# A graph layer on one core: transform the second half of the batches to frequencies on two row groups of TensorE

## The chip, the cores and the metric

The kernel runs on one core of a Trainium2 chip. The metric is the device time of one execution in microseconds; the kernel before takes 1838.17 us (median of four runs, 1836.39 to 1841.95). A core has TensorE (matmuls, in the profile PE, and its weight loads, PEld), VectorE (DVE), ScalarE (ACT), GpSimd (POOL) and SyncE (SP, which here only issues DMAs). ScalarE and POOL issue DMAs too. All data are 32-bit floats.

## The reference

For 32 batches of 512 tokens and 256 features the layer normalises the rows, `h = max(layernorm(x), 0)`, and computes from `h`, cut to what matters here:

```python
g = relu(bn1(conv1(h)))              # 1x1 convolution over the channels
g = bn2(conv2(g))                    # 17 taps along the tokens, 256 -> 256 channels
x_conv = relu(g + h)
s = h @ w_se.T + b_se                # 3 features
A = exp(-dist(s, s)) * adj           # 512 x 512 per batch
x_nmp = A @ relu(h @ w_msg.T + b_msg)
r, z, n = gru_gates([x_conv, x_nmp], h)
out = x + (1 - z) * n + z * h
```

The convolution with 17 taps is done in frequencies: the tokens are cut into windows of 64, each is transformed to 80 real numbers, multiplied by the transformed taps and transformed back.

## The kernel before

The batches form two groups of 16. `V = 64` is the window, `L = 80` the numbers per transformed window, `W = 8` the windows of a batch, so one group fills 128 columns (`W * GB`) of a tile `xf` of 128 channels x 2 channel halves x 80 frequencies x 128 windows.

The work runs in five stages: the first part for group 0 (0 to about 160 us), the node stage of group 0 (messages, distances, aggregation, with the products of the frequencies between), the first part for group 1 (about 456 to 576 us), the node stage of group 1, and the gates for all pairs of batches (from about 870 us).

`first_part(g, ...)` (from L806) is a loop over the batches of a group, written by hand inside `manual_schedule`, so the order of the calls is the order on each engine's queue. Per batch b it runs, in a skewed pipeline: `statistics(b + 2)` and `normalise(b + 2)` on VectorE with a power on POOL, `transpose_h(b + 1)` (8 transposes on TensorE, L311, two evictions on VectorE, L315, a DMA to HBM), `conv1(b)` (8 matmuls of 256 columns, each two passes in the trace, L327; VectorE adds the shift, L330; ScalarE does the relu, L331) and `windows_to_freq(b - 1)`.

`windows_to_freq` (L335 to L346) takes, for each half of the channels, four blocks of 128 tokens as weights, `H1[b][:, c, ...]` (128 tokens x 128 channels), and multiplies them by the constant `fwd`, 128 x 160. `fwd` is block diagonal: rows 0 to 63 with columns 0 to 79 transform the even window, rows 64 to 127 with columns 80 to 159 the odd window. Two blocks share a PSUM bank, and ScalarE copies it, four windows of 80, into `xf` (L345).

In group 0 the loop also transforms the taps. `weights_to_freq` (L245 to L269) is one of 32 steps: four matmuls of 17 rows, 80 weight columns and 512 columns, one on each row group of 32 rows (L255), each into a bank of its own; the banks are copied to SBUF, two or three of the four by ScalarE (L265), the others by VectorE (L263), and every second step four DMAs on SP's queue store them to HBM (L269). Which engine copies which bank depends on the place of the step in its group of four input channels: in a step that begins such a group VectorE takes banks 1 and 3, in the other it takes bank 3 alone. `load_taps` loads the inputs of four steps, on POOL's queue.

`between(b)` gives the steps of a batch and `slot()` places them: for most batches one step after the transposes and one after `conv1`, with a third after `windows_to_freq` in two batches; batch 1 has none of its own and does what batch 0 left. Every PSUM tile is one of 8 banks, given out in turn, so a matmul waits until the copies of the bank's last user are done. Group 1 has no taps; there `between` gives sums of the gates' weights on POOL and ScalarE.

The gates end with `last_z` for the last pair of batches, whose output is stored by four DMAs of 128 KB for the first batch and two times four of 64 KB for the second, by turns on SP's and ScalarE's queues (`store`, L808).

Of the kernel before, what the change touches and what calls it, by code (L numbers as in the profile page):

```python
# [15 lines left out]
P = 128  # L16
# [8 lines left out]
V = 64  # L25
# [40 lines left out]
def gnn_layer(  # L66
# [268 lines left out]
    def windows_to_freq(b, xf):  # L335
        w0 = (b % GB) * W
        per = 2
        for ic in range(DC):
            for c0 in range(0, NC, per):
                p = bank(f"px_{b}_{ic}_{c0}")  # L340
                for j in range(per):
                    nc.tensor.matmul(p[:, j * 2 * L : (j + 1) * 2 * L], H1[b][:, c0 + j, ic * P : (ic + 1) * P],  # L342
                                     fwd, start=True, stop=True)
                w = w0 + 2 * c0
                nc.scalar.copy(xf[:, ic, :, w : w + 2 * per],  # L345
                               p[:, : per * 2 * L].rearrange("p (w f) -> p f w", f=L))  # L346
        del H1[b]
# [62 lines left out]
    def load_h(b):  # L410
        HT[b] = work.tile([P, DC, N], FP, tag="hT", name=f"hT2_{b}")
        nc.sync.dma_start(HT[b], HD[b])
# [240 lines left out]
    def last_z(p, terms):  # L653

        d, o, ks = RZ[p], 1, range(K3)

        def gated(src, other, i, j, t=slice(0, N)):
            z, g = d[:, DC + i, j, t], DC + i
            if other is not None:
                nc.vector.tensor_add(z, other[:, t], src[:, t])  # L660
                src = z
            nc.scalar.activation(z, src, AF.Sigmoid, bias=brz[:, g : g + 1], scale=1.0)

        def places(i, t):
            return slice(t.start // 32, t.stop // 32), slice(32 * i, 32 * (i + 1))

        def turned(i, j, t=slice(0, N)):
            dst, (js, half) = d[:, i, j, t], places(i, t)
            nc.vector.tensor_mul(dst, dst, d[:, DC + i, j, t])
            if (p, j) not in OUT:  # L670
                OUT[p, j] = pools["late"].tile([P, N // 32, D // 4], FP, tag="o", name=f"o_{p}_{j}", bufs=2)
            nc.vector.transpose(OUT[p, j][:, js, half], dst.rearrange("p (j k) -> p j k", k=32))

        def added(i, j, t=slice(0, N)):
            js, half = places(i, t)
            x = XP[p][j][:, js, half]
            nc.vector.tensor_add(x, x, OUT[p, j][:, js, half])


        ts = [slice(h * N // 2, (h + 1) * N // 2) for h in range(2)]  # L680
        b1, b2, b4, *b3 = (bank(f"pz{k}_{p}") for k in range(1, 6))
        into(b1, Q1, o, ks, terms, True)
        p1 = temp("p1", f"z{p}")
        nc.scalar.copy(p1, b1)
        into(b2, Q6, o, ks, terms, True)
        u2 = temp("u2", f"z{p}")
        nc.vector.tensor_add(u2, p1, b2)
        into(b1, Q2, o, ks, terms, False)
        gated(b1, None, 0, 0)
        early_out(p, 1, 1)  # L690
        turned(0, 0)
        into(b2, Q7, o, ks, terms, False)
        u3 = temp("u3", f"z{p}")
        nc.vector.tensor_add(u3, p1, b2)
        early_out(p, 0, 1)
        added(0, 0)
        for bk, t in zip(b3, ts):
            into(bk, Q5, o, ks, terms, True, t)
            gated(bk, u3, 1, 1, t)
        into(b4, Q4, o, ks, terms, True)  # L700
        turned(1, 1)
        added(1, 1)
        gated(b4, u3, 1, 0)
        for bk, t in zip(b3, ts):
            into(bk, Q3, o, ks, terms, False, t)
            gated(bk, u2, 0, 1, t)
            if t is ts[0]:
                turned(1, 0)
        added(1, 0)
        store(p, 0, [nc.sync, nc.scalar])  # L710
        for t in ts:
            turned(0, 1, t)
            added(0, 1, t)
            store(p, 1, [nc.sync, nc.scalar], t)
# [100 lines left out]
    def first_part(g, freq, between, left=()):  # L815


        b0, b1 = g * GB, (g + 1) * GB
        for b in range(b0, b0 + 3):
            if b not in X and (g == 0 or b == b0):  # L820
                load_x(b)
        if g == 0:
            t = XN[b0] = pools["first"].tile([P, NC, D], FP, tag="xn", name="rows", bufs=2)
            ones, diags = t[:, 0, :P], t[:, 1:3, :].rearrange("p i (c m) -> p i c m", m=P)
            nc.vector.memset(ones, 1.0)

            for _ in range(5):
                nc.tensor.matmul(row1[1][:, : 2 * P], ident, fr.rearrange("p c g k -> p (c g k)")[:, : 2 * P], start=True, stop=True)
            batch_norm("bn1", scale1, shift1, nc.gpsimd)
            bn1_row(0, scale1, ones, diags)  # L830
            bn1_row(1, shift1, ones, diags)
        if b0 not in STATS:
            statistics(b0)
        normalise(b0)
        if g == 0:
            scale_w1()
            shift_w1()
        left = list(left)

        def fill():  # L840
            for step in left.pop(0) if left else ():
                step()

        if g > 0:
            load_x(b0 + 1)
            fill()
            load_x(b0 + 2)
        transpose_h(b0)
        fill()
        statistics(b0 + 1)  # L850
        if g > 0:
            statistics(b0 + 2)
        normalise(b0 + 1, g > 0)
        fill()
        for b in range(b0, b1):
            if b + 3 < b1:
                load_x(b + 3, nc.gpsimd)
            if b == b0:
                conv1(b)
                one, two = between(0) if g == 0 else ([], [])  # L860
                for step in one:
                    step()
                fill()
                if g == 0:
                    transpose_h(b + 1)
                    statistics(b + 2)
                    normalise(b + 2)
                else:
                    normalise(b + 2)
                    transpose_h(b + 1)  # L870
                fill()
                xf, last_two = freq(g), two
                continue
            if g == 0:

                slots = last_two if b == b0 + 1 else between(b - b0)

                def slot():
                    for step in slots.pop(0) if slots else ():
                        step()  # L880

                if b == b0 + 1:
                    between(b - b0)
                    conv1(b)
                    slot()
                if b == b0 + 2:
                    slot()
                if b == b1 - 1:
                    load_h(b0)
                if b + 2 < b1:  # L890
                    statistics(b + 2)
                if b + 1 < b1:
                    transpose_h(b + 1)
                if b > b0 + 2:
                    slot()
                if b + 2 < b1:
                    normalise(b + 2)
                if b > b0 + 1:
                    conv1(b)
                    slot()  # L900
                if b == b1 - 1:
                    by_chunks(b)
                    load_h(b0 + 1)
                windows_to_freq(b - 1, xf)
                slot()
                continue
            if b + 2 < b1:
                statistics(b + 2)
            if b + 1 < b1:
                transpose_h(b + 1)  # L910
            if b + 2 < b1:
                normalise(b + 2)
            one, two = between(b - b0)
            conv1(b)
            if b == b1 - 1:
                load_h(b0)
            for step in one:
                step()
            windows_to_freq(b - 1, xf)
            for step in two:  # L920
                step()
        if g > 0:
            by_chunks(b1 - 1)
            load_h(b0 + 1)
        windows_to_freq(b1 - 1, xf)
        by_chunks(b0)
        return xf
# [8 lines left out]
    with tc.tile_pool(name="freq", bufs=1) as fpool:  # L936
# [3 lines left out]
        with phase("first", "gen"):  # L940
# [10 lines left out]
            nc.scalar.dma_start(fwd, nc.inline_tensor(fwd_np, name="dft_fwd").ap())  # L951

            def between(b):
                if 1 <= b <= len(load_weights):
                    load_weights[b - 1]()

                n = (2, 0, *(3 if b in (6, 11) else 2 for b in range(2, GB)))[b]
                mine = [[steps.pop(0)] for _ in range(n)]
                if b % 2 == 0 and b // 2 + 1 < QI // PI:
                    mine[b > 0].insert(0, partial(load_taps, gen, b // 2 + 1))  # L960
                return (mine[0], mine[1:]) if b == 0 else mine

            with tc.manual_schedule():
                xf = first_part(0, freq_tile, between)
# [159 lines left out]
```

## Time and profile before

| what | value |
|---|---|
| four runs | median 1838.17 us, 1836.39 to 1841.95 |
| the profiled execution | 1841.95 us, span 1840.2 us |
| granted TensorE clock | 0.995 of full speed |
| first part, group 0 (0 to 160 us) | TensorE busy 153.67 us, VectorE 119.65, ScalarE 85.52, DMA 0.90 |
| node stage, group 0 (160 to 456 us) | TensorE busy 292.79 us of 296, DMA 0.79 |
| first part, group 1 (456 to 576 us) | TensorE busy 120.00 us of 120, VectorE 97.64, ScalarE 50.50, DMA 0.69 |
| node stage, group 1 (576 to 870 us) | TensorE busy 293.28 us of 294, DMA 0.83 |
| gates (870 to 1840 us) | TensorE busy 958.60 us of 970, DMA 0.35 |

The profiled execution is one of the four runs, and the slowest of them. In the lines that follow, a timeline line gives the start in us, the length in us from the first start to the last end of a run of equal instructions, engine, line, operation and tiles, how many, and in brackets the idle time before it with what ended it. A busy TensorE is no proof of full use, since matmuls are pipelined and overlap in the records: the distance from one start to the next is the better measure. A line of instructions by tile gives how many and the shortest, median and longest duration in ns.

### The profile page before, as it was taken

The page shows a single profiled execution, that of the slowest core. Times are in us where ns is not written, and L with a number is a line of the kernel's source. Part 1 is how long each engine was busy: PE and PEld are TensorE (multiplying, and loading weights), DVE is VectorE, ACT ScalarE, POOL GpSimd, SP SyncE. Part 2 cuts the span into 40 slices and gives each one's busy share as a digit, 9 for nine tenths or more (in the row PEclk, how much of TensorE's full clock was granted, in tenths as well). Part 3 has the DMA queues.
Part 4 walks back from the last instruction along what each step waited for, and adds up shares of the span by engine and source line. Part 5 has one row for each costly group of instructions (what it writes and reads, how often), then busy time and mean ns, then how long its engine had stood idle before and what let it go on. Part 6 is the DMA issues. An engine that isn't in the chain of part 4 may idle for free.

```text
span 1840.2 us, 20110 instructions
## 1 busy us (share of the span) xinstructions
PE 1818.3 (99%) x6614; PEld 1083.9 (59%) x6614; DVE 1107.5 (60%) x2220; ACT 583.5 (32%) x1084; POOL 590.5 (32%) x572
## 2 busy tenths in 40 slices
PE   8999999999999999999999999999999999999997
PEld 6776666666897766675545554555445554555443
DVE  7884556554896555454266456654666456655666
ACT  4555343432345333333212221222122221222121
POOL 3431233334432444444331332123221323133221
PEclk9999999999999999999999999999999999999999
DMA  9998789775678987877432344224422443234412
GB/s 238 312 294 225 224 239 240 201 205 182 202 250 202 261 254 217 231 209 235 113 100 50 90 120 120 71 50 120 120 86 36 119 120 103 56 82 120 120 26 44
DMA packets 307500, 289.26 MB, mean 157 GB/s; under 512 B 148076, under 2 KB 237196, under 8 KB 307012
## 3 DMA queue, kind: packets, MB, share of 16 engines
q1 hardware_dynamic: 281380, 224.22, 45.8%
q10 hardware_dynamic: 18992, 38.68, 5.9%
q0 software_dynamic: 7024, 25.07, 4.5%
q8 instruction: 53, 0.87, 0.2%
q14 instruction: 51, 0.42, 0.1%
HBM read 191.50 MB, written 96.40 MB: 156 GB/s over the span
## 4 chain that ended last, share of the span: by engine, by line
PE 91%; DMA 3%; DVE 2%; issue 1%; ACT 1%; POOL 1%; SPq 0%; ACTq 0%; DVEq 0%; POOLq 0%
PE pg L601 30%; PE pn L601 15%; PE pn L491 12%; PE py L392 11%; PE pc L327 5%; PE pm L439 5%; PE pc L589 5%; PE px L342 3%; PE pd L476 2%; PE pw L255 1%; PE phT L311 1%; DMA adj<-in_adj_dram 1%; PE pz L601 1%; DMA x<-in_x_dram 1%; PE psr L465 1%
## 5 line engine op out<-in xcount | busy, mean ns | idle before, releaser
L491 PE MATMUL pn<-A,msg 128*128 128x512 f32 x512 | 227.4, 597 | 2.5 <-ACT e L479 2.1
L601 PE MATMUL pg<-hp,sw 128*128 128x512 f32 x434 | 221.8, 593 | 0.7 <-DVE rz L620 0.5
L601 PE MATMUL pg<-cp,sw 128*128 128x512 f32 x434 | 221.6, 592 | 0.0
L601 PE MATMUL pg<-np,sw 128*128 128x512 f32 x434 | 221.6, 592 | 0.0
L579 POOL TENSOR_TENSOR hp<-hp 128x512 f32<-128x512 f32 x64 | 81.3, 1281 | 414.4 <-DMA hp<-hd 295.3
L491 PEld LDWEIGHTS pn<-A,msg 128*128 128x128 f32 x512 | 97.4, 191 | 114.0 <-issue 106.8
L371 POOL TENSOR_TENSOR both<-xf 128x256 f32<-128x256 f32 x78 | 60.0, 769 | 324.9 <-PE py L392 290.4
L579 POOL TENSOR_TENSOR cp<-cp 128x512 f32<-128x512 f32 x64 | 80.5, 1268 | 228.0 <-ACT cp L595 226.8
L392 PE MATMUL py<-wt,both 128*128 128x256 f32 x624 | 152.4, 387 | 0.3 <-ACT e L479 0.3
L616 ACT ACTIVATE rz<-rz,brz 128x512 f32<-128x512 f32 x93 | 67.0, 721 | 260.2 <-DVE rz L620 260.2
L399 DVE TENSOR_TENSOR y<-y,py 128x256 f32<-128x256 f32 x78 | 31.8, 408 | 186.3 <-ACT y L398 186.3
L601 PEld LDWEIGHTS pg<-hp,sw 128*128 128x128 f32 x434 | 82.2, 190 | 104.8 <-issue 98.3
L601 PEld LDWEIGHTS pg<-np,sw 128*128 128x128 f32 x434 | 82.5, 190 | 103.8 <-issue 103.8
L601 PEld LDWEIGHTS pg<-cp,sw 128*128 128x128 f32 x434 | 82.5, 190 | 103.8 <-issue 103.8
L392 PEld LDWEIGHTS py<-wt,both 128*128 128x128 f32 x624 | 115.1, 192 | 43.4 <-issue 27.6
L482 DVE TENSOR_TENSOR A<-e,at 128x512 f32<-128x512 f32 x128 | 115.4, 940 | 34.7 <-ACT e L479 34.5
L358 POOL TENSOR_TENSOR wsum<-wt 128x512 f32<-128x512 f32 x78 | 108.7, 1395 | 54.7 <-DMA wt<-wd 42.8
L327 PE MATMUL pc<-w,hT 128*128 128x256 f32 x512 | 119.5, 387 | 1.5 <-DVE hT L315 1.5
L739 ACT ACTIVATE nt<-nt,vech 128x512 f32<-128x512 f32 x64 | 46.2, 722 | 235.8 <-DVE nt L738 235.8
L439 PE MATMUL pm<-wmsg,hq 128*128 128x259 f32 x512 | 117.5, 381 | 0.0
L601 PE MATMUL pn<-np,sw 128*128 128x512 f32 x224 | 114.4, 592 | 0.0
L601 PE MATMUL pn<-hp,sw 128*128 128x512 f32 x224 | 114.4, 592 | 0.0
(145 smaller groups left out, 2945.6 us busy)
## 6 DMA issues: line engine op xcount, KB each, us to landing
wt<-wd SPq DMA_DIRECT2D x160, 256.0 KB, 4.5
adj<-in_adj_dram SPq DMA_DIRECT2D x128, 256.0 KB, 5.6
wd<-wst SPq DMA_DIRECT2D x64, 320.0 KB, 6.0
yd<-y ACTq DMA_DIRECT2D x80, 256.0 KB, 4.2
yt<-yd SPq DMA_DIRECT2D x30, 640.0 KB, 7.4
hd<-hT SPq DMA_DIRECT2D x32, 512.0 KB, 4.4
nd<-nmp ACTq DMA_DIRECT2D x32, 512.0 KB, 4.4
xb<-in_x_dram SPq DMA_DIRECT2D x128, 128.0 KB, 3.8
```

The lines of the kernel that those rows point to most:

```text
L327: nc.tensor.matmul(p[:, j, :], HT[b][:, ic, c * P : (c + 1) * P], w1[:, ic, :], start=(ic == 0), stop=(ic == DC - 1))
L342: nc.tensor.matmul(p[:, j * 2 * L : (j + 1) * 2 * L], H1[b][:, c0 + j, ic * P : (ic + 1) * P], fwd, start=True, stop=True)
L358: nc.gpsimd.tensor_tensor(t, WT[g, u][:, 0], WT[g, u][:, 1], op=ALU.add)
L371: nc.gpsimd.tensor_tensor(both[:, 0], re, im, op=ALU.add)
L392: nc.tensor.matmul(dst, v[:, ic, :], w[:, ic, :], start=(ic == 0), stop=(ic == DC - 1))
L439: nc.tensor.matmul(p[:, : D + NS], hq[:, ic, c * P : (c + 1) * P], wmsg[:, ic, :], start=(ic == 0), stop=(ic == DC - 1))
L482: nc.vector.tensor_mul(A[b][:, mc, :], e, at)
L491: nc.tensor.matmul(p, MSG[b][:, mc, dc * P : (dc + 1) * P], A[b][:, mc, :], start=(mc == 0), stop=(mc == NC - 1))
L579: nc.gpsimd.tensor_tensor(t[:, dst, :], t[:, a, :], t[:, b, :], op=sub)
L589: nc.tensor.matmul(bk[:, t0:t1], YT[p][j][:, c, oc * P : (oc + 1) * P], back[:, n : n + t1 - t0], start=(c == 0), stop=(c == len(spans) - ...
L601: nc.tensor.matmul(bk[:, t], sw[:, k, q, o, :], terms[k][q][:, t], start=(first and i == 0), stop=(i == len(ks) - 1), skip_group_check=True)
L616: nc.scalar.activation(rz[:, g, j, :], src, AF.Sigmoid, bias=brz[:, g : g + 1], scale=1.0)
```

## The change

Three things change.

In group 1 (b of 16 or more) `windows_to_freq` takes each half of a token block by itself: 64 rows of `H1` as weights, 80 columns of `fwd`, rows 0 to 63 into one bank for the even windows and rows 64 to 127 into another for the odd ones. Per half of the channels there are eight matmuls of 64 rows and 80 columns by turns on the two row groups in place of four of 128 rows and 160 columns. ScalarE copies each bank once, into every second window of `xf`. Group 0 keeps the old matmuls.

In group 0 the slots are gone. Both groups run one loop body: statistics, transposes, normalise, `conv1`, the first step of the batch, `windows_to_freq`, the other steps. The 32 steps are spread over 15 batches (two each, three in batches 7 and 14, none in batch 15), the last `by_chunks` and `load_h` come after the loop in both groups, and `load_taps` is called before the steps of every even batch.

In `last_z` the four stores of the last pair's first batch all go to SP's queue.

```diff
     def windows_to_freq(b, xf):
         w0 = (b % GB) * W
         per = 2
-        for ic in range(DC):
+        for ic in range(DC) if b >= GB else ():
+
+            ps = [bank(f"px_{b}_{ic}_{k}") for k in range(2)]
+            for c in range(NC):
+                for k, p in enumerate(ps):
+                    rows = slice(V * k, V * (k + 1))
+                    nc.tensor.matmul(p[:, c * L : (c + 1) * L], H1[b][rows, c, ic * P : (ic + 1) * P],
+                                     fwd[rows, k * L : (k + 1) * L], start=True, stop=True)
+            for k, p in enumerate(ps):
+                nc.scalar.copy(xf[:, ic, :, w0 + k : w0 + W : 2],
+                               p[:, : NC * L].rearrange("p (w f) -> p f w", f=L))
+        for ic in range(DC) if b < GB else ():
             for c0 in range(0, NC, per):
...
-        store(p, 0, [nc.sync, nc.scalar])
+        store(p, 0, [nc.sync])
...
-            if g == 0:
-
-                slots = last_two if b == b0 + 1 else between(b - b0)
...
-                windows_to_freq(b - 1, xf)
-                slot()
-                continue
+            if g == 0 and b == b0 + 1:
+                conv1(b)
+                for step in last_two:
+                    step()
             if b + 2 < b1:
                 statistics(b + 2)
             if b + 1 < b1:
                 transpose_h(b + 1)
             if b + 2 < b1:
                 normalise(b + 2)
             one, two = between(b - b0)
-            conv1(b)
+            if b > b0 + (g == 0):
+                conv1(b)
             if b == b1 - 1:
                 load_h(b0)
             for step in one:
                 step()
             windows_to_freq(b - 1, xf)
             for step in two:
                 step()
-        if g > 0:
-            by_chunks(b1 - 1)
-            load_h(b0 + 1)
+        by_chunks(b1 - 1)
+        load_h(b0 + 1)
         windows_to_freq(b1 - 1, xf)
...
             def between(b):
+                if b % 2 == 0 and b // 2 + 1 < QI // PI:
+                    load_taps(gen, b // 2 + 1)
                 if 1 <= b <= len(load_weights):
                     load_weights[b - 1]()
-
-                n = (2, 0, *(3 if b in (6, 11) else 2 for b in range(2, GB)))[b]
-                mine = [[steps.pop(0)] for _ in range(n)]
-                if b % 2 == 0 and b // 2 + 1 < QI // PI:
-                    mine[b > 0].insert(0, partial(load_taps, gen, b // 2 + 1))
-                return (mine[0], mine[1:]) if b == 0 else mine
+                mine = spread(steps, b, GB - 1) if b < GB - 1 else []
+                return mine[:1], mine[1:]
```

More of the change, by code (lines that the diff above doesn't have):

```diff
@@ L873, in first_part @@
                 continue
-            if g == 0:
-                slots = last_two if b == b0 + 1 else between(b - b0)
[L878 to L883, printed above, removed]
-                    conv1(b)
-                    slot()
[L886 to L902, printed above, removed]
-                    load_h(b0 + 1)
-                windows_to_freq(b - 1, xf)
-                slot()
-                continue
+            if g == 0 and b == b0 + 1:
+                conv1(b)
+                for step in last_two:
+                    step()
             if b + 2 < b1:
@@ L913, in first_part @@
             one, two = between(b - b0)
-            conv1(b)
+            if b > b0 + (g == 0):
+                conv1(b)
             if b == b1 - 1:
@@ L921, in first_part @@
                 step()
-        if g > 0:
-            by_chunks(b1 - 1)
-            load_h(b0 + 1)
+        by_chunks(b1 - 1)
+        load_h(b0 + 1)
         windows_to_freq(b1 - 1, xf)
```

## The prediction

> **What bounds the kernel now.** I read the page first: engine totals and the chain of work that ended last.
>
> ```profile
> span 1840.2 us, 20110 instructions
> PE 1818.3 (99%) x6614; PEld 1083.9 (59%) x6614; DVE 1107.5 (60%) x2220; ACT 583.5 (32%) x1084; POOL 590.5 (32%) x572
> PE 91%; DMA 3%; DVE 2%; issue 1%; ACT 1%; POOL 1%; SPq 0%; ACTq 0%; DVEq 0%; POOLq 0%
> ```
>
> TensorE is the bound, so a microsecond counts where the TensorE stream gets shorter or gets a new hole. Second, the frequency matmuls by tile (px), the edited step:
>
> ```profile
> L342 PE MATMUL px<-fwd,h x512: 299/299/403, 26.4 to 572.5; 128*128 128x160 f32 x171
> L345 ACT COPY xf<-px x128: 406/438/485, 27.9 to 573.0; 128x320 f32<-128x320 f32 x128
> ```
>
> The file has 256 such matmuls and the trace 512: each runs as two passes. The longest record is 403 ns, 104 more than the median: a first pass that had to wait for its weights. So a load of 128 columns costs about 0.104 us when nothing hides it. Third, the timeline of the second group (482 to 490 us):
>
> ```profile
> 483.08 2.34 PE L342 MATMUL px<-fwd,h 128*128 128x160 f32 x16
> 485.26 1.04 PE L311 MATMUL phT<-ident,xn 128*128 128x128 f32 x8
> 489.59 2.34 PE L342 MATMUL px<-fwd,h 128*128 128x160 f32 x16
> ```
>
> Read start to start: px to phT is 2.18 us for 16 passes, 0.136 each, and a batch is 6.51 us without a hole. Fourth, matmuls that already use row groups, the distances (pd, 9 rows by 128 columns of weights) and the taps (pw, 17 rows, 80 columns), and around the taps the first group's engines (79 to 93 us):
>
> ```profile
> 235.39 0.31 PEld L476 LDWEIGHTS pd<-sr,sl 9*128 9x128 f32 x8 [0.34 <-issue]
> ```
> ```profile
> 81.25 1.37 DVE L303 TENSOR_SCALAR xn<-x,mv,rstd 128x256 f32<-128x256 f32 x4
> 82.54 1.28 DVE L330 TENSOR_TENSOR h<-pc,shift_row 128x512 f32<-128x512 f32 x2
> 82.61 1.10 PE L255 MATMUL pw<-w2p,taps 17*80 17x512 f32 x8
> 83.25 1.23 ACT L331 ACTIVATE h<-h 128x512 f32<-128x512 f32 x2 [2.66 <-DVE h L330]
> 83.64 2.44 PE L342 MATMUL px<-fwd,h 128*128 128x160 f32 x16
> 85.03 1.39 DVE L284 BATCH_NORM_STATS2 stats<-x 128x6 f32<-128x256 f32 x4
> 85.92 1.04 PE L311 MATMUL phT<-ident,xn 128*128 128x128 f32 x8
> 86.34 0.36 DVE L286 BATCH_NORM_AGGREGATE mv<-stats 128x2 f32<-128x6 f32 x4
> 86.74 0.17 DVE L289 TENSOR_SCALAR rstd<-mv 128x4 f32<-128x4 f32 x1
> 86.82 1.29 DVE L315 TENSOR_SCALAR hT<-phT 128x512 f32<-128x512 f32 x2
> 88.00 1.55 ACT L265 COPY wst<-pw 80x512 f32<-80x512 f32 x3 [1.27 <-PE pw L255]
> 91.57 1.10 PE L255 MATMUL pw<-w2p,taps 17*80 17x512 f32 x8
> ```
>
> Eight passes of 512 columns take 1.03 us (82.61 to 83.64), while one 512-column pass of the gate product takes 0.43 us (36.05 us for 84 on the chain): the four row groups do run side by side. Taps to taps, 82.61 to 91.57, is one batch, 8.96 us: 2x1.03 taps, 2.28 px, 0.96 transposes, 3.65 convolution. TensorE has no hole here either.
>
> **The change part by part.** All against the profiled execution's own time, 1841.95 us (span 1840.2, 1.75 around it). That run is the slowest of the four; the median, 1838.17, is 3.78 lower, and I carry the difference over to it.
>
> **1. Frequencies by row groups, 16 batches.** Removed per batch: 16 passes, 2.18 us. Added: 32 passes of 80 columns in two row groups, 16 each. Passes cost 0.43/512 per column, so 80 columns are 0.069 us; but each pass needs its own 128 columns of weights. In the pd row eight loads on four row groups end 0.31 us after the first starts; one of them is recorded with 0.183 (the median by tile), so the last starts about 0.125 after the first. Taking off the 0.02 by which the four groups are staggered, a row group's second load starts about 0.105 to 0.107 after its first: loading 128 columns sets the pace, not the matmul. 16x0.107+0.07 = 1.78 us, the first load included. Changing between whole-array and row-group work costs about 0.09 on entry (the taps of 91.57 could have started at 91.48: 87.92, a bare first load of 0.104, and 16 passes of 0.216, by 3.46 us for 16 on the chain), and 0.19 on leaving (1.03 less 0.07 for 80 columns of load and 2x0.43 leaves some 0.09, and the next first load is bare again, 0.104): 1.78+0.28 = 2.06. Gain 0.12 a batch. About ten of the batches run at 6.50 us; the rest start 6.8 to 7.0 apart, waiting for normalised rows from VectorE, and gain nothing there: **-1.2 us**. Bounds: with no price for changing, -0.40x16 = -6.4; with the two row groups one after the other, 32x0.107+0.28-2.18 = +1.5x16 = +24. I take the low price, since pd and pw show loads and passes side by side.
>
> The skill's page "TensorE: Matmul & The Clock Gate" (Part 3, The mechanism) speaks against the change: a load overlaps a running matmul only in another row group. Then each row group would pay load plus pass, and by that rule this part would be +14.8 us instead of -1.2. The px rows disagree: passes on all rows start 0.136 apart, with the 0.104 load hidden. The page "TensorEngine Tiling (Array Packing)" (Theoretical Speedup) gives up to twice the speed for 64 rows; that would be -17 us, and it leaves out the load.
>
> The four evictions a batch stay four of 320 elements (0.44 us), now writing every second window; each pair starts when an input-channel half is complete. ScalarE is busy 50 of the 120 us of this stage, so even doubled they are hidden; the last pair ends about 0.3 us later, under 3.5 us of message matmuls.
>
> **2. The first group's order goes back.** The same matmuls, evictions and DMAs, but the 32 taps steps move: before, one after the transposes and one after the convolution; now one between convolution and px, the other after px, 2 a batch (3 in batches 7 and 14, none in 15). SP's weight stores and POOL's taps loads move with them; POOL's loads no longer wait for the step in hand. What is late next is a ring through four engines. The step after px reuses the four banks of the step before it (12 banks back to back, 8 in all), so it waits for ScalarE's copies; these queue behind the relu, which waits for VectorE's shift addition; and VectorE is behind its copy of the previous late step. From VectorE's last copy: statistics 1.31 (85.03 to 86.34), aggregates 0.40, rstd 0.08, transposes out 1.21, normalise 1.29 (81.25 to 82.54), additions 1.28, relu 0.63 less 0.09 overlap, three ScalarE copies 1.55, TensorE 1.10, VectorE's copy 0.60, five hand-overs of 0.03 to 0.05: 9.5 us against 8.96. That is where the early step is one of which ScalarE copies three banks; after batch 7 it always is. Before batch 7 ScalarE copies two, the ring is 9.0, and nothing is lost. Seven batches by 0.55: **+3.9**. Bounds: 0, if hand-overs overlap more than I read; +9, if VectorE's operations follow one another with no overlap (0.08 at each of five changes, 0.4 more in all 13 batches). The beginning, where batch 1 now has steps of its own: +0.4 (0 to +1).
>
> **3. Start of the node stage.** The last weight store no longer comes in batch 15, so weight loads and the mask behind them on SP's queue start earlier relative to the last px. There VectorE waited 2.40 us for the mask at 179.24 and TensorE about 2 us to 181.80. DMA is busy throughout, so I take **-0.5** (0 to -3.8).
>
> **4. Final store on one queue.**
>
> ```profile
> 1831.57 4.91 SPq L808 DMA_DIRECT2D out_dram<-xb  x6
> 1831.58 5.07 ACTq L808 DMA_DIRECT2D out_dram<-xb  x6
> ```
>
> Six issues each now become eight on SP and four on ScalarE. SP's 0.43 an issue puts its first four at 1831.6 to 1833.0; its later ones, as the changed program is built, reuse DMA semaphores and wait for earlier landings (3.4 us in the DMA view), so its last goes at about 1837.6 instead of 1836.4: **+1.2** (0 to +2).
>
> Sum: -1.2+3.9+0.4-0.5+1.2 = **+3.8**: 1845.8 for the profiled execution, 1842.0 from the median.
>
> **The rivals.** *Faster:* the ring stays under 8.96 (part 2 costs 0) and changing modes is free: -6.4-0.5+1.2 = -5.7, 1832.5. It decides if the ring is 0.5 us shorter than I add up, for which speaks that VectorE's rows overlap by 0.08 each; against it, that the taps rows show the 0.09. *Hidden:* the ring's delay is given back at the mask load: 3.9 becomes about 0 net, 1838 to 1839. For it: DMA is 90% busy in the first 160 us. Against: the chain there is TensorE's. *The packing does not pack:* the 64-row loads go one after the other, 1838.2+24+5 = 1867; or load and pass alternate, +14.8+5: 1858. Against: pd and pw.
>
> **How the numbers follow.** Ring as added up, +0.5 to +8: 0.62, of it 0.40 over 0.2% (3.7 us, about what a measurement of this kernel tells from no change). Hidden: 0.18, 0.15 of it within 0.2%. Faster: 0.11. No packing: 0.09. So slower 0.49, same 0.38, faster 0.13. The range leaves out the packing failure and the far end of the faster case: 1836 to 1850.
>
> **What would show it.** Right: taps-to-taps about 9.5 us from batch 8 on, with TensorE holes before the step after px put down to ScalarE's copies; px blocks of about 1.8 us from first load to last pass start and batches of 6.4 in the second group. Wrong: loads of one row group much under or over 0.107 apart, holes absent, or px blocks over 2.5 us.

## The result, and the profile after

The changed kernel takes 1840.71 us (median of 47 runs, 1836.31 to 1845.44) against 1837.60 us for the kernel before (median of 70, 1833.61 to 1845.48). The ratio is 1.0015, with a 95% interval of 1.001 to 1.002: some 2.8 us, or 0.15%, longer. That is inside the 0.2% that the prediction called no change, a case to which it gave 0.38 (0.49 went to a kernel slower by more), and 1.3 us below the 1842.0 that it named.

The profiled executions alone would mislead. The one of before took 1841.95 us, 4.3 us over the median of its kernel, and the one of after 1839.89 us, 0.8 us under its own. Their difference, -2.1 us, has the wrong sign. So in what follows times are compared by the repeated runs, and the profiles only stage by stage.

The page of the changed kernel, span, engine totals and the chain of work that ended last, by engine:

```profile
span 1838.1 us, 20618 instructions
PE 1817.7 (99%) x6870; PEld 1079.1 (59%) x6870; DVE 1106.9 (60%) x2220; ACT 582.7 (32%) x1084; POOL 587.9 (32%) x572
PE 65%; issue 1%; DVE 1%; POOL 1%; ACT 0%; DVEq 0%; POOLq 0%; ACTq 0%
```

TensorE has 256 records more (6614 to 6870), 16 more in each of 16 batches, and the other engines do the same work as before. TensorE, busy 99%, is still the bound. The chain's 65% is no effect of the change: a second profile of the kernel before (`before_again`, below) shows the same line, where the first had 91%.

The second group, instructions by tile (px) and the timeline from 481 to 488 us:

```profile
L344 PE MATMUL px<-fwd,h x512: 272/272/333, 475.0 to 568.5; 64*128 64x80 f32 x171
L353 PE MATMUL px<-fwd,h x256: 299/299/474, 26.1 to 163.4; 128*128 128x160 f32 x128
L347 ACT COPY xf<-px x64: 414/440/467, 478.8 to 569.7; 128x320 f32<-128x320 f32 x64
```
```profile
481.42 1.86 PEld L344 LDWEIGHTS px<-fwd,h 64*128 64x128 f32 x32 [0.33 <-issue]
483.37 1.09 PE L311 MATMUL phT<-ident,xn 128*128 128x128 f32 x8
487.85 2.02 PE L344 MATMUL px<-fwd,h 64*128 64x80 f32 x32
```

From the first load of a block to the transposes is 1.95 us. Before, it was 2.18 from the first pass, whose load ran beside the convolution. From block to block it is 6.43 (6.51 before). The eviction that writes every second window costs what the old one did, 440 ns.

The first group, timeline from 111 to 122 us, one batch and the beginning of the next:

```profile
111.79 1.10 PE L255 MATMUL pw<-w2p,taps 17*80 17x512 f32 x8
112.42 1.29 DVE L330 TENSOR_TENSOR h<-pc,shift_row 128x512 f32<-128x512 f32 x2
113.14 1.23 ACT L331 ACTIVATE h<-h 128x512 f32<-128x512 f32 x2 [4.64 <-DVE h L330]
114.28 1.53 ACT L265 COPY wst<-pw 80x512 f32<-80x512 f32 x3
115.19 1.76 PE L255 MATMUL pw<-w2p,taps 17*80 17x512 f32 x8
116.50 1.28 DVE L263 COPY wst<-pw 80x512 f32<-80x512 f32 x2 [2.20 <-PE pw L255]
117.70 1.39 DVE L284 BATCH_NORM_STATS2 stats<-x 128x6 f32<-128x256 f32 x4
119.49 1.29 DVE L315 TENSOR_SCALAR hT<-phT 128x512 f32<-128x512 f32 x2
120.79 1.47 DVE L303 TENSOR_SCALAR xn<-x,mv,rstd 128x256 f32<-128x256 f32 x4
121.36 1.10 PE L255 MATMUL pw<-w2p,taps 17*80 17x512 f32 x8
122.18 1.28 DVE L330 TENSOR_TENSOR h<-pc,shift_row 128x512 f32<-128x512 f32 x2
```

Read it as a ring. VectorE adds (112.42), ScalarE does the relu (113.14) and only then copies the early step's banks (114.28), so the late step after the frequencies (115.19) is stretched from 1.10 to 1.76 us, two matmuls at a time; VectorE copies its banks (116.50), and everything after that on VectorE follows without a gap to the next addition (122.18). VectorE's only wait is the 2.20 us for the late step. The view of waits names the releaser (60 to 160 us):

```profile
PEld pw L255 <- ACT wst L265: 2.0, 8, 0.3
```

Taps to taps is 9.57 us here (111.79 to 121.36), where it was 8.96.

Third, the start of the node stage (before, then after), TensorE and the transposed mask:

```profile
178.72 1.03 PE L392 MATMUL py<-wsum,xf 128*128 128x256 f32 x4
179.24 1.30 DVE L481 STREAM_TRANSPOSE at<-adj 128x512 f32<-128x512 f32 x2 [2.40 <-DMA adj<-in_adj_dram]
181.80 8.83 PE L491 MATMUL pn<-A,msg 128*128 128x512 f32 x16 [2.06 <-ACT e L479]
```
```profile
179.91 1.30 DVE L492 STREAM_TRANSPOSE at<-adj 128x512 f32<-128x512 f32 x2
181.88 1.03 PE L403 MATMUL py<-wsum,xf 128*128 128x256 f32 x4
182.74 7.03 PE L502 MATMUL pn<-A,msg 128*128 128x512 f32 x16
```

The kernel before waits 2.40 us for the mask and TensorE 2.06 us for what follows from it. After the change the mask is there in time and both waits are gone. What the first group loses, this stage returns in part. (That the 16 matmuls take 7.03 us and not 8.83 is no part of it: in the profile of before the granted clock was 0.50 from 183.0 to 186.4 us, and the second profile has 7.13.)

The stages, by the distance between first starts of a tile (TensorE; us):

| stretch | before | before, second profile | after |
|---|---|---|---|
| first transposes of group 0 to its first message matmul | 151.89 | 149.42 | 154.94 |
| first message to first aggregation matmul | 21.37 | 21.59 | 19.23 |
| first to second aggregation | 22.62 | 19.28 | 20.01 |
| one batch, second group, without a wait | 6.50 | 6.50 | 6.42 |
| start of the last matmul to the last instruction's end | 11.20 | 11.26 | 11.50 |

Against the first profile of before that is +3.1 in the first group, -2.1 at the start of the node stage and +0.3 at the end, against the second +5.5, -2.4 and +0.2. The first group is uncertain since the clock differs there: it was 0.50 for 3.4 us in the changed kernel (from 26.4 us) and in the first profile of before (from 19.1), and never in the second.

### The profile page after: what moved, and what is told of

Same layout as the page of the kernel before. It is cut to its first block, busy times and chain, and to the rows that moved or that the text cites. A ratio compares the mean times of both kernels' runs of the same rounds, so it can differ in the third digit from the quotient of the medians.

```text
span 1838.1 us, 20618 instructions
## 1 busy us (share of the span) xinstructions
PE 1817.7 (99%) x6870; PEld 1079.1 (59%) x6870; DVE 1106.9 (60%) x2220; ACT 582.7 (32%) x1084; POOL 587.9 (32%) x572
## 4 chain that ended last, share of the span: by engine, by line
PE 65%; issue 1%; DVE 1%; POOL 1%; ACT 0%; DVEq 0%; POOLq 0%; ACTq 0%
PE pg L612 30%; PE pn L612 15%; PE pn L502 6%; PE py L403 6%; PE pc L600 5%; PE pm L450 2%; PE pd L487 1%; PE pz L612 1%; PE psr L476 0%; DVE A L493 0%; POOL cp L590 0%; POOL nt L802 0%; POOL rz L801 0%; DVE at L492 0%; DVE rz L680 0%
## 5 line engine op out<-in xcount | busy, mean ns | idle before, releaser
L612 PE MATMUL pn<-cp,sw 128*128 128x512 f32 x224 | 114.4, 592 | 0.0
```

The costliest lines, as they stand in the source:

```text
L612: nc.tensor.matmul(bk[:, t], sw[:, k, q, o, :], terms[k][q][:, t], start=(first and i == 0), stop=(i == len(ks) - 1), skip_group_check=True)
```

## The experiments

Each ratio is to runs of the kernel before on the same chip and beside it, with its 95% interval; 0.001 is 1.84 us.

**The change in its three parts.** First the frequencies of the second group alone (the first hunk of the change), in `rows_only`.

> The kernel before with the row groups in the second group alone, nothing else changed. Theory A (the three parts act as the prediction has them): 0.08 to 0.15 us saved in each of 16 batches, 1.2 to 2.4 us less than before; a block of px, first load to the next first load, 1.9 to 2.0 us against 2.18. Rival B (the second group pays for the change of array mode): equal or slower, px blocks of 2.2 us or more, batches of 6.5 us.

Measured: 1838.27 us, ratio 1.0002 (0.9992 to 1.0013). The block is 1.95 us and an undisturbed batch 6.42 us, so TensorE does save 0.08 us a batch; the time doesn't show it. In its profile several batches start 6.6 to 7.1 us apart, with VectorE's statistics waiting 3.7 us in all for tokens that are still on their way and the transposes for the normalised rows.

The order of the taps' steps alone (all hunks in `first_part` and `between`), in `order_only`.

> The kernel before with the taps steps in the new order alone (the first group's loop, by_chunks and between as in the change). Theory A: 3 to 5 us more than before, batches of 9.5 to 9.7 us from batch 8 on, TensorE held before the late step by ScalarE's copies. Rival C (what the batches lose is given back at the start of the node stage, as the two profiled executions suggest, where the second aggregation begins 1.6 us earlier after the change than before it): within 1 us of before, with batches just as long.

Measured: 1839.77 us, ratio 1.0016 (1.0007 to 1.0025), +2.9 us. This part alone gives as much as the whole change. From batch 8 on its batches are 9.57 to 9.75 us apart, as in the changed kernel.

The last stores alone, in `store_only`:

```diff
-        store(p, 0, [nc.sync, nc.scalar])
+        store(p, 0, [nc.sync])
```

> The kernel before with the four stores of the last pair's first batch all on SP's queue. Theory A as predicted: 1.2 us more. Rival D (the two profiled executions: from TensorE's last matmul to the end 10.9 us before and 11.1 after): 0.2 to 0.3 us more.

Measured: 1836.88 us, ratio 1.0004 (0.9993 to 1.0015): not to be told from nothing. From the start of the last matmul to the end of the last instruction it takes 11.45 us (11.20 before). In all three profiles with the new stores this is 11.42 to 11.50 us, in all eleven with the old ones 10.98 to 11.29, so the traces speak for some 0.3 us.

**The ring, cut.** `order_early` is `order_only` with the early step of the first group ahead of the convolution:

```diff
+            if g == 0:
+                for step in one:
+                    step()
             if b > b0 + (g == 0):
                 conv1(b)
             if b == b1 - 1:
                 load_h(b0)
-            for step in one:
-                step()
+            if g > 0:
+                for step in one:
+                    step()
             windows_to_freq(b - 1, xf)
```

> The new order of the taps' steps alone (frequencies and stores as before), but in the first group the early step of a batch stands ahead of the convolution and no longer between the convolution and the frequencies; the late step stays after the frequencies. The late step then reuses two banks of the early step, copied out before the relu and not behind it, and the two of the convolution. Theory (a ring of four engines: the late step waits for ScalarE's copies, these for the relu, this for VectorE's additions): the ring is cut, batches 8 to 11 of the first group come down from 9.5-9.7 to 8.9-9.1 us, the late step takes 1.1 us again, and the time is that of the kernel before within 1.5 us, about 2 to 3 us under that of the order alone (1839.8 in the earlier comparison). Rival 1 (the place of the late step or the transfers that move with it cost the time): batches stay at 9.5-9.7, time stays 1.5 to 3 us over the kernel before. Rival 2 (ScalarE's early copies now make the relu late): batches over 9.5 with the hole ahead of the frequencies, 1841 or more.

Measured: 1834.11 us, ratio 0.9986 (0.9978 to 0.9995), -2.6 us. The timeline of this kernel at 121 us:

```profile
121.15 1.23 ACT L331 ACTIVATE h<-h 128x512 f32<-128x512 f32 x2 [3.49 <-DVE h L330]
121.85 1.10 PE L255 MATMUL pw<-w2p,taps 17*80 17x512 f32 x8
```

The late step runs while the relu is still going, takes 1.10 us again, and the batches from the tenth on are 8.9 to 9.2 us apart. So the ring was the cause of the 9.6. Two things were not expected. The time ended below the kernel before, not at it. By the trace that is the start of the node stage, which keeps its shorter 19.05 us and no longer has to pay for a ring. And the batches before, 9.0 to 9.5 us apart, did not come down; what holds them is another wait, at the step that was moved (1.3 to 1.6 us there), and was not followed further.

**The ring, made longer.** `ring_longer` is `order_only` with all four banks of the early step copied by ScalarE:

```diff
-    def weights_to_freq(gen, pc, i):
+    def weights_to_freq(gen, pc, i, early=False):
...
-            if (pc or i >= SI) and (q == 3 or (q == 1 and s == 0)):
+            if not early and (pc or i >= SI) and (q == 3 or (q == 1 and s == 0)):
...
             for step in one:
-                step()
+                step(True) if g == 0 else step()
```

> The new order of the taps' steps alone, with one thing more: in the early step of each batch of the first group ScalarE copies all four banks and VectorE none. Theory (ring): three ScalarE copies of 0.52 us in the ring become four, so batches from 8 on go from 9.5-9.7 to 10.0-10.3, and the earlier ones rise by 0.5 to 1.0; some 7 x 0.5 + 5 x 0.6 = +6.5 us against the order alone, 1845 to 1848. Rival 1 (VectorE's sum of work sets the pace): VectorE loses 0.6 us a batch, batches come down to 9.0-9.1, 1835 to 1838. Rival 2 (delays of the first group are given back at the transfers before the node stage): batches grow, but the time stays within 1.5 us of the order alone, 1838.5 to 1841.5.

Measured: 1846.32 us, ratio 1.0053 (1.0039 to 1.0066). Nearly every batch from the fourth on is 10.0 to 10.1 us, although VectorE was relieved of at least one copy a batch (busy 67% of the time from 60 to 151 us, 78% in `order_only`):

```profile
118.83 1.23 ACT L331 ACTIVATE h<-h 128x512 f32<-128x512 f32 x2 [4.63 <-DVE h L330]
119.96 2.02 ACT L265 COPY wst<-pw 80x512 f32<-80x512 f32 x4
120.88 2.23 PE L255 MATMUL pw<-w2p,taps 17*80 17x512 f32 x8
```

One copy more (1.53 to 2.02 us) makes the late step 2.23 us instead of 1.76 and the batch 10.05 instead of 9.6: nearly the same amount three times. The rival that VectorE's sum of work sets the pace fell.

**Less work off the ring.** `rows_both` is the kernel before with the 64-row frequencies in both groups; `after_rows_both` is the changed kernel with them in both groups. The edit is the same:

```diff
-        for ic in range(DC) if b >= GB else ():
+        for ic in range(DC):
...
-        for ic in range(DC) if b < GB else ():
-            for c0 in range(0, NC, per):
```

> The kernel before with the row groups in both groups of batches. In the first group px stands behind a taps step, so its first load is bare already and the array changes its mode there anyway. Theory A: 0.2 to 0.3 us saved a batch in the first group on top of the second group's 0.1, 4 to 7 us less than before, batches of 8.7 us. Rival E (the first group is paced by ScalarE, VectorE or DMA as soon as TensorE gets shorter): no more than the second group alone gives, 1 to 2 us less.

Measured: 1833.24 us, ratio 0.9983 (0.9971 to 0.9994), -3.1 us where 4 to 7 less were expected, with batches of 8.68 where they were 8.96. Where TensorE sets the pace of the first group, work taken off it counts.

> The changed kernel with the 64-row frequencies in both groups. In the old order this took 0.27 us off each batch of the first group (8.96 to 8.69). Theory (a ring of four engines, not TensorE's work, sets the first group's pace in the new order; the frequencies are not in the ring): batches 8 to 13 stay at 9.5-9.75 us, the holes ahead of the late step grow by what the frequencies lose, and the time is within 1 us of the changed kernel's (1840 to 1841), 2 us or more over the kernel before. Rival (TensorE's own sequence with a little waiting sets the pace): batches 9.2 to 9.45, 0.27 x 14 = 3.8 us less than the changed kernel, 1836.5 to 1837.5.

Measured: 1843.84 us, ratio 1.0036 (1.0023 to 1.0048). The same edit, now in the new order, made the kernel slower than the changed one by 3 to 4 us. That the ring would hide the gain was expected; batches of 10.2 us, from transposes to transposes, were not. Windows of half a microsecond around one batch (busy TensorE, granted clock, DMA share, GB/s) and TensorE's timeline there:

```profile
131.00:131.50 0.50, 0.50 (x4) 1.00 0.91 246
131.50:132.00 0.50, 0.50 (x5) 0.67 0.95 238
132.00:132.50 0.50, 0.50 (x4) 0.50 0.87 287
...
134.50:135.00 0.50, 0.50 (x3) 0.50 0.77 229
135.00:135.50 0.50, 0.50 (x3) 0.92 0.25 82
135.50:136.00 0.50, 0.50 (x5) 1.00 0.04 16
```
```profile
128.33 1.12 PE L344 MATMUL px<-fwd,h 64*128 64x80 f32 x14 [0.15 <-DVE h L330]
129.38 2.14 PE L255 MATMUL pw<-w2p,taps 17*80 17x512 f32 x8
131.44 1.80 PE L311 MATMUL phT<-ident,xn 128*128 128x128 f32 x8
133.04 4.63 PE L327 MATMUL pc<-w,hT 128*128 128x256 f32 x16
```

Every second batch the granted clock is 0.50 from about 131.7 to 135.0 us, some 3.4 us, and the transposes (1.80 for 1.09) and the convolution (4.63 for 3.62) run through it. From 70 to 156 us there are five such stretches, which begin 20.48 us apart; two batches take 20.3 to 20.4 us. From 100 us on, from late step to late step, the batches alternate between 9.2 us, without such a stretch, and 11.1 to 11.2 with one. The 9.2 is below the 9.57 of the changed kernel, so this run does not show that the ring hides the gain: the clock took back whatever came through, and more.

**The pace of a row group.** `rows_wide` is `rows_only` with 128 columns streamed per pass instead of 80, the extra 48 unused:

```diff
-                    nc.tensor.matmul(p[:, c * L : (c + 1) * L], H1[b][rows, c, ic * P : (ic + 1) * P],
-                                     fwd[rows, k * L : (k + 1) * L], start=True, stop=True)
+                    nc.tensor.matmul(p[:, c * P : (c + 1) * P], H1[b][rows, c, ic * P : (ic + 1) * P],
+                                     fwd[rows, k * (2 * L - P) : k * (2 * L - P) + P], start=True, stop=True)
```

> The kernel before with 64-row frequencies in the second group, each pass streaming 128 columns instead of 80 (48 of them are computed and not used). Theory (loading 128 columns of weights, about 0.11 us, sets the pace of a row group, a pass of 128 columns by 0.43/512 takes 0.107 and lies beside the next load): a block of 32 passes stays at 1.95 us from the first load to the next transposes, at most +0.1; time within 1.5 us of the kernel before. Rival 1 (load and pass of a row group follow one another, 0.104+0.069 before, 0.104+0.107 now, or the pass sets the pace): the block grows by 16 x 0.04 = 0.6 us, batches 7.0 us, +9 us in time.

`rows_serial` is `rows_only` with the loops over blocks and row groups exchanged, so that eight passes of one row group follow one another:

```diff
-            for c in range(NC):
-                for k, p in enumerate(ps):
-                    rows = slice(V * k, V * (k + 1))
+            for k, p in enumerate(ps):
+                rows = slice(V * k, V * (k + 1))
+                for c in range(NC):
```

> The kernel before with 64-row frequencies in the second group, the matmuls of an input-channel half in another order: all eight passes of the upper 64 rows, then all eight of the lower 64 rows, so that two neighbours are mostly on the same row group; same loads, passes and evictions. Theory (the two row groups run side by side, each at its own load's pace of about 0.11 us): one after the other they take 32 x 0.11 + 0.2 = 3.7 us a block instead of 1.95, less at the three changes between row groups; batches 8.0 to 8.2 us, 14 x 1.7 = +24 us, 1858 to 1864. Rival 1 (a 64-row load costs half, and the loads follow one another anyway): the block stays at 1.95 to 2.2 us, time within 3 us of the kernel before. Rival 2 (a load may not overlap a pass of its own row group): 32 x (0.104+0.069) = 5.5 us a block, +50 us.

Weight loads of a block, from the timelines of `rows_only`, `rows_wide` and `rows_serial`:

```profile
509.96 1.86 PEld L344 LDWEIGHTS px<-fwd,h 64*128 64x128 f32 x32 [0.33 <-issue]
```
```profile
509.06 1.86 PEld L344 LDWEIGHTS px<-fwd,h 64*128 64x128 f32 x32 [0.33 <-issue]
```
```profile
508.38 2.51 PEld L344 LDWEIGHTS px<-fwd,h 64*128 64x128 f32 x32 [0.33 <-issue]
```

`rows_wide` measured 1834.89 us, ratio 0.9992 (0.9983 to 1.0001): 60% more columns cost nothing in the loads' pace, 1.86 us again, and 0.04 us at the end of a block. The loads set the pace, as the prediction had it. In single records of `rows_only` the loads of the two row groups start 6 or 7 ns apart, and those of one row group 108 to 112 ns apart.

`rows_serial` measured 1846.49 us, ratio 1.0053 (1.0037 to 1.0068); the block is 2.59 us, the batch 7.06. That lies between the theories. Single records point to why: the first five and the last five loads of a block are 108 to 112 ns apart, and those between come mostly in pairs, 38 to 44 and 67 to 73 ns apart, together 0.111 again. The records do not name the row group; read by their spacing, a row group alone keeps to 0.11 us a load, and TensorE starts work of the second row group before that of the first has ended, though it stands behind it in the program. That was not in the expectation.

**A second profile of before**, `before_again`.

> The kernel before, unchanged, for a second profile of it. The profiled execution shown was the slowest of its four; its first group has one batch of 11.46 us among batches of 8.96. If that is a stray wait of this execution, the second profile has no batch over 10.1 us there, and an own time of 1837 to 1839; if it belongs to the kernel, the same batch is long again.

It took 1834.93 us. The long batch is there again, 11.13 us at the same place, so it belongs to the kernel. (In all seven profiles with the old order it takes 10.4 to 12.3.) It is a batch with a third step, which stands behind the frequencies, as the late step of the change does. In both profiles of before this third step takes 2.12 us instead of 1.10 (from 74.85 us in the first, where the trace puts the wait down to ScalarE's copies). So the kernel before had the same wait in one batch. What differed between the two were dips of the clock: three of 3.4 us in the first profile, from 19.1, 183.0 and 200.0 us, and none in the second before its last matmuls. TensorE at the first aggregation (178 to 190 us; busy us and records of PE, PEld, DVE, ACT and POOL, then granted clock, DMA share, GB/s), before and second profile:

```profile
178.00:190.00 12.00, 9.94 (x24) 4.73 (x23) 9.31 (x16) 3.35 (x6) 1.41 (x2) 0.86 0.96 193
```
```profile
178.00:190.00 12.00, 10.91 (x37) 6.64 (x38) 7.75 (x14) 4.92 (x10) 1.35 (x2) 1.00 0.86 196
```

**The parts put together.** `early_rows_both` and `early_rows_g2` are `order_early` with the 64-row frequencies in both groups, and in the second alone.

> The new order with the early step ahead of the convolution (which cut the ring: first-group batches of 8.9 us) and the 64-row frequencies in both groups. Theory (with the ring cut TensorE's own sequence sets the pace, so work taken off it counts): batches 9 to 14 of the first group come down by the 0.27 us that the frequencies lose, 8.9 to 8.65; about 11 x 0.27 = 3 us less than with the order alone moved ahead, 5 to 6 us under the kernel before, a ratio of 0.9970 (0.9958 to 0.9982). Rival (the chain through VectorE and ScalarE is right behind TensorE): batches stay at 8.9, or a dip of the granted clock follows the new holes as it did in the changed kernel with 64-row frequencies in both groups; ratio 0.9985 to 1.003.

Measured: 1836.73 us (1830.64 to 1838.83), ratio 0.9995 (0.9984 to 1.0005). The time is the rival's, though in the profile, one of the two fastest runs, batches of 8.9 to 9.2 us came down to 8.7 to 9.1. The twelve runs part by their granted clock: the two at 0.998 took 1830.64 and 1830.76 us, those at 0.993 to 0.995 took 1835.1 to 1838.8.

> The same order with the early step ahead of the convolution, and the 64-row frequencies in the second group only. What the second group's 64-row frequencies are worth, against the order alone moved ahead (ratio 0.9986): by TensorE's count 0.08 us in 16 batches, 1.2 us or 0.0007; theory (VectorE's normalised rows, which wait for the tokens' loads, take most of it back, as in the run of this part alone, ratio 1.0002): 0 to -0.6 us, ratio 0.9983 to 0.9987. Rival (the gain was there and only hidden in scatter): -1.2 us, ratio 0.9979.

Measured: 1834.59 us, ratio 0.9982 (0.9974 to 0.9991), -3.3 us against before and 0.0004 under `order_early`. What the second group's 64-row frequencies are worth by themselves stays open: the three kernels with them stand at +0.0002 (alone), -0.0004 (against `order_early`) and -0.0008 (`rows_wide`), each uncertain by 0.001; 16 x 0.08 us would be -0.0007.

`early_rows_g2`, `order_early` and `rows_both` lie below the kernel before with their whole intervals, by 0.14 to 0.18%.

## Why the prediction was right, point by point

The forecast of +3.8 us became +2.8 (1.8 to 3.7). The mechanism was the one named, the ring. Terms 3 and 4 were mis-sized, both too high, by some 2.8 us together: with their measured sizes the same sum would have been +1.0. That the named time was met so well is in part luck, since terms 1 and 2 gave some 1.8 us more than they said, and how much of that is whose stays open.

| term | predicted | measured |
|---|---|---|
| 1, row groups, second group | -1.2 (0.12 a batch) | 0.08 a batch; +0.4, -0.7 and -1.5 us in three comparisons, not resolved |
| 2, ring, seven batches | +3.9 | +4.0 by the traces; with the ring cut the whole kernel is 5.5 us shorter, uncertain by some 2 (ratios 1.0016 and 0.9986) |
| 2, beginning | +0.4 | not separable; the whole first group is 3.1 to 5.5 us longer |
| 3, start of the node stage | -0.5 | -2.1 to -2.4 |
| 4, last stores | +1.2 | +0.3 by the traces, +0.7 with an interval of -1.3 to +2.8 by time |

**Term 1.** The pace of the loads, side by side in two row groups, is shown: 0.112 us where 0.107 was taken. From the first load to the start of the last pass a block takes 1.75 (about 1.8 predicted). The entry costs 0.093 (last pass of the convolution to the first of the block is 0.309 us instead of 0.216; 0.09 predicted). The sum, 2.06 predicted, comes out at 2.10: 1.95, the entry, and the 0.06 that the second pass of the transposes starts late. The bound of +24 us, one row group after the other, was far off: even `rows_serial`, where the row groups follow one another in the program, costs 0.64 us a block more, and 9 us in all. As to the skill's page "TensorE: Matmul & The Clock Gate" (Part 3, The mechanism), weighed in the prediction: the loads in `rows_wide` keep their 0.112 us though the passes got longer, so a load and a pass of one row group do overlap here. The factor two of "TensorEngine Tiling (Array Packing)" would have needed a block of 1.1 us; the block is 1.95.

**Term 2.** Taps to taps of about 9.5 us from batch 8 on was predicted; 9.56 to 9.75 was measured. The difference, 0.1 to 0.2, fits VectorE's copy behind the late step: after the last of ScalarE's three copies (115.81) it takes 1.97 us to the end of VectorE's second copy (117.78), where 1.10 for TensorE and 0.60 for a copy were added. The seven batches from batch 7 on, one of them with a third step in either kernel (10.39 us in the changed one), take 68.3 us between their transposes, where both profiles of before take 64.3. "Before batch 7 nothing is lost" was wrong: there batches are 9.1 and 9.5 in turn, against 8.96. The holes stand where they were announced, before the late step, put down to ScalarE's copies.

**Term 3** was the one most mis-sized. The direction and the bound (-3.8) were right, but the term was set low since the DMA queues are busy throughout. By the traces the stores leave earlier, counted from the first message matmul: the last weight store is issued 1.9 us before it in both profiles of before, 4.4 in the changed kernel, and the first load of the mask 6.6 us after it in both profiles of before, 3.6 in the changed kernel. The stretch from the first message to the first aggregation is 19.0 to 19.7 us in all seven profiles with the new order, against 20.9 to 21.6 in all seven with the old. The stores were not moved by themselves. `order_early`, which has this gain and no ring, shows it in the time.

**Term 4** was too large. The last issue does go later: SP's run of stores ends 8.8 us after the start of the last matmul, where ScalarE's ended 7.7 us after it in before, +1.1 for the +1.2 predicted. But the landing gives most of it back. The last stores of before, then of after (KB each, median us from issue to landing):

```profile
out_dram<-xb SPq DMA_DIRECT2D x4, 64.0 KB, 3.4
out_dram<-xb ACTq DMA_DIRECT2D x4, 64.0 KB, 4.1
```
```profile
out_dram<-xb ACTq DMA_DIRECT2D x4, 64.0 KB, 3.3
out_dram<-xb SPq DMA_DIRECT2D x4, 64.0 KB, 1.9
```

The last stores land sooner in these rows, and the end moved by 0.3.

**The rivals.** *Hidden* (the ring's delay given back at the mask load, 1838 to 1839) was half right: some 2 us come back there, but not because the ring is late, since `order_early` has them without the ring. *Faster* fell with the ring's 9.6. *The packing does not pack* fell with the block of 1.95.

## What to carry to other kernels

In this kernel a step put behind another that uses the same PSUM banks inherited the whole chain that frees these banks. Add up that chain around all engines before moving a step, for here one ScalarE copy more in it was 0.5 us in every batch, and moving the step ahead of the convolution cut it. Ask of every reordered loop also what its last transfer was holding up, for a loop that ends its stores a batch earlier can pay at the next stage's first load. And look at the granted clock before calling work taken off TensorE a gain: the same edit gave -0.28 us a batch in one order and a slower kernel in the other, where the clock fell in every second batch.

## What was not expected of the hardware

**The clock falls by half for some 3.4 us without a long idle time.** In `after_rows_both` the clock was 0.50 in five stretches of about 3.4 us from 70 to 156 us, and before the one shown TensorE had only 17-row and 64-row matmuls, with waits of 0.15 to 0.3 us between them (125.7 to 131.4 us). The Trainium skill's page "TensorE: Matmul & The Clock Gate" (HAM oscillation — how this bites in real kernels) gives as the rule that no idle gap may exceed about 3.4 us. The two levels and the length agree with the rows; the rule does not cover them, since no gap in the stretch shown came near that. `ring_longer` has longer holes in its late step (2.23 us for 1.10) and 128-row frequencies, and shows no dip from 66 to 150 us. In the three kernels with 64-row frequencies in both groups the median clock of the runs is 0.993 (`after_rows_both`), 0.9945 (`early_rows_both`) and 0.9965 (`rows_both`), where the runs of before beside them have 0.997; of the other kernels only `rows_serial`, with four runs, is under that (0.996). This speaks for the rows in use rather than the sum of the holes, but neither was tried by itself.

**These dips go with much of the scatter of this kernel.** Half the clock for 3.4 us costs up to 1.7 us and lowers the mean clock of the run by about 0.001. Of the 29 runs of before beside `rows_wide`, those at 0.998 took 1833.3 to 1834.5 us (and one 1839.3), those at 0.996 took 1836.8 to 1839.2. The same wait may bring a dip or not: TensorE's 1.9 to 2.1 us before the first aggregation were followed by one in `before` (183.0 us) and `rows_only` (181.0), and by none in `before_again` and `store_only`.

**TensorE works on the second row group before the first is done**, as the spacing in `rows_serial` is read above, and two 64-row loads run side by side, 6 or 7 ns apart, at no loss to each other: 0.112 us from load to load of a row group, 0.111 where one runs alone.
